# Mamba scan steps by turns in both channel halves, a gather of two 64-column products, three DRAM copies of the rows, and layer 1 in the same steps

## The chip, the cores and the metric

The kernel runs on one core of a Trainium2 chip, with its five engines: TensorE (PE, whose weight loads are shown as PEld), VectorE (DVE), ScalarE (ACT), GpSimd (POOL) and SyncE (SP, which here only issues DMAs). The metric is the device time in microseconds. Before the change it is 8173.62 us, the median of three runs (8168.15 to 8188.78).

## The reference: what is computed

An image x of two batches, 64 channels and 96 x 96 points goes through four layers:

- layer 0: attention over all 9216 points of a batch, added to x
- layer 1: depthwise and 1x1 convolutions, batch norm and ReLU; then a Mamba block over the 9216 points of each batch as one sequence
- layer 2: four Mamba blocks over the image's columns and rows (96 sequences of 96 points each way and batch, once forwards and once backwards), each direction pair joined by a linear layer
- layer 3: a 3 x 3 filter whose taps come from the image's mean

The change is in the Mamba blocks of layers 1 and 2. A block has 128 inner channels d and 16 states s. In each point t:

```
dt = softplus(...)                     # per channel and point
h[d,s] = exp(dt[d] * A[d,s]) * h[d,s] + dt[d] * B[s] * x[d]
y[d]   = sum over s of h[d,s] * C[s]  + x[d] * Dp[d]
```

B and C are the same for all channels of a point; dt and x the same for all states of a channel. In layer 1 h runs on from chunk to chunk; in layer 2 it starts from zero in each sequence. All is float32.

## The kernel before

**Units and steps.** A unit is one Mamba block on 768 points of one batch: 24 units in layer 1 (a chunk of 768 points each, with a carried state), 96 in layer 2 (eight sequences of 96 points, one direction; a forward and a backward unit of the same points follow each other and share the normalised input). 128 channels times 16 states are 2048 recurrences; 128 partitions hold 128 of them, so a unit has 16 steps. Partition p belongs to state p // 8 and, in step n, to channel (8n + p) mod 128: a step is eight channels for each state, and every step shifts the channels by eight partitions. (HALF = 384 points, CH = 768, STEPS = 16.)

**How the channels are shifted.** `step_write` (L821) writes the unit's tile dtu (128 channels x 1536: dt, and e = dt times x) to DRAM twice, one copy below the other, in two DMAs of 768 KB. `read` (L839) then fetches the 128 rows from row 8n on: the second copy makes the wrap. The SBUF tile that receives them is named spread; there are six, and a read is issued five steps ahead.

**One step of a unit.**

- `decay` (L849), ACT, three steps ahead: h = exp(dt times a rate per partition)
- `inputs` (L868), DVE: e times B into the PSUM tile place
- `scan` (L879): the DVE scan along the points, then on POOL h times C
- `gather` (L895), PE, two steps late: a 128 x 128 matrix of zeros and ones, a shifted window of the tile pair, sums the states of a channel into the PSUM tile low; one product per half of the points. Before the first of them a product with `direct` puts x times Dp there.
- `shared` (L859), PE: the product that gives B, in PSUM

Layer 1 (`carry` set) takes all 768 points of one group n in a step: one read of 768 KB, one decay, one scan whose first value is the carried state, which POOL copies back, and B in the tile that layer 2 uses for its second place. Layer 2 (`paired`) takes two groups n = 2m, 2m+1 on one half of the points in a step: steps 0 to 7 are the first half, 8 to 15 the second. It reads two blocks of 384 KB, has two decays of 384 points, and works out the inputs of two steps ahead of their two scans. In both layers a step has two gather products of 384 points.

**The other pieces of a unit** are worked in between. The list PIECES in `Mamba` gives each an offset in steps from the unit's step 0, and `run` (L998) issues, for every step: the read, the decay, inputs and scan, `shared`, the gather, then the pieces due. Every engine and the SP queue work their own instructions in exactly this order. The pieces that matter below, by the step at which they come up, whatever unit is being stepped through (call it j):

- 1, 5, 7, for unit j+1: `step_sum`, `step_dt`, `step_u` (POOL, L808, L811, L815): they finish dt and e. 8: `step_write` of them (SP, L824). From step 11 on the reads are those of unit j+1.
- 7, 9, for unit j+2: `conv_read` and `gate_read` (ACT, L765 and L772 to L774). 11, 13: `step_mm` (PE) and `step_read` (ACT, L791 and L792). 14: `step_exp` (ACT, L796 to L798). 15: `step_kept` (POOL, L805).
- 10: `y_half` (ACT, L915), which frees low for the second half of unit j. 3: `y_gate` (POOL, L926) of unit j-1.

So while unit j is stepped through, the dt and e of unit j+1 are finished, written out and read back shifted, and those of unit j+2 begun.

**DMA completions.** The SP queue's DMAs take eight completion semaphores in turn: a DMA is issued only when the one eight places before has landed.

Of the kernel before, what the change touches and what calls it, by code (L numbers as in the profile page):

```python
# [523 lines left out]
def mamba_tables(k, pool):  # L524

    nc = k.nc
    G = P // 8
    t = SimpleNamespace()  # L530

    t.member = pool.tile([P, 8], FP, name="member")
    nc.vector.reduce_sum(t.member, k.ident.rearrange("p (g i) -> p i g", i=8), axis=AX.X)
    t.group = pool.tile([P, 2, G], FP, name="group")
    for j in range(2):
        nc.vector.reduce_sum(t.group[:, j], k.ident.rearrange("p (g i) -> p g i", i=8), axis=AX.X)

    t.turned = pool.tile([P, G, G], FP, name="turned")
    two = t.group.rearrange("p j g -> p (j g)")
    for n in range(G):  # L540
        nc.vector.tensor_copy(t.turned[:, n], two[:, G - n : 2 * G - n])

    pair = pool.tile([P, 2, P], FP, name="pair")
    nc.vector.tensor_copy(pair, k.ident.unsqueeze(1).to_broadcast([P, 2, P]))
    pair = pair.rearrange("p j c -> p (j c)")
    t.gather = [pair[:, P - 8 * n : 2 * P - 8 * n] for n in range(G)]

    t.centre = pool.tile([P, P], FP, name="centre")
    nc.vector.tensor_sub(t.centre, k.ident, k.mean_c)
    return t  # L550
# [8 lines left out]
def mamba_weights(k, w, pool, product, tables, i):  # L559
# [15 lines left out]
    p = product(tables.placed.rearrange("p s i -> p (s i)"), tables.group[:, 0], P, G)  # L575
# [38 lines left out]
class Mamba:  # L614
# [14 lines left out]

    STEPS = P // 8  # L630
# [3 lines left out]
    def __init__(self, k, tables, wk, dram, ps, ps_m):  # L634
        self.k, self.nc, self.t = k, k.nc, tables
        self.wk, self.dram, self.ps_m = wk, dram, ps_m


        self.places = [self.wide(ps.tile([P, 2 * NB], FP, name=f"place{i}")) for i in range(2)]
        self.low = [ps.tile([P, NB], FP, name=f"low{i}")[:, :HALF] for i in range(2)]  # L640
# [141 lines left out]
    def step_read(self, u):  # L782
        nc = self.nc

        u.both = self.work("dtu", 2 * CH, bufs=1)
        order = "p (j a t) -> p a j t" if u.paired else "p (a j t) -> p a j t"
        both = u.both.rearrange(order, a=2, j=2)
        u.dt, u.e = both[:, 0], both[:, 1]
        u.kept = self.by_half(self.work("kept", bufs=1))
        p = self.by_half(u.p)  # L790
        nc.scalar.activation(u.e, p, AF.Abs, bias=u.w.dt_b)  # L791
        nc.scalar.activation(u.dt, p, AF.Relu, bias=u.w.dt_b)  # L792
# [28 lines left out]
    def step_write(self, u):  # L821
        u.rows = self.dram.tile([2 * P, 2 * CH], FP, tag="rows", name="rows")
        for j in range(2):
            self.nc.sync.dma_start(out=u.rows[j * P : (j + 1) * P], in_=u.both)  # L824
# [10 lines left out]
    def paired(self, step):  # L835
        half, m = divmod(step, self.STEPS // 2)
        return half, (2 * m, 2 * m + 1)

    def read(self, u, step):  # L839
        u.dtu[step] = self.work("spread", 2 * CH, bufs=6)  # L840
        if not u.paired:
            self.nc.sync.dma_start(out=u.dtu[step], in_=u.rows[8 * step : 8 * step + P])
            return
        half, groups = self.paired(step)
        for q, n in enumerate(groups):
            row = u.rows[8 * n : 8 * n + P, bass.ts(half, CH)]
            self.nc.sync.dma_start(out=u.dtu[step][:, bass.ts(q, CH)], in_=row)

    def decay(self, u, step):  # L849

        h = u.h[step] = self.work("h", bufs=9)
        if not u.paired:
            self.nc.scalar.activation(h, u.dtu[step][:, :CH], AF.Exp, scale=u.w.rates[:, step : step + 1])  # L853
            return
        for q, n in enumerate(self.paired(step)[1]):
            dt = u.dtu[step][:, q * CH : q * CH + HALF]
            self.nc.scalar.activation(h[:, bass.ts(q, HALF)], dt, AF.Exp, scale=u.w.rates[:, n : n + 1])  # L857

    def shared(self, u, half=0):  # L859

        if u.paired:
            sides, halves = [self.low[0]], [half]
        else:
            (sides, u.B), halves = self.places[1], range(2)
        for j, p in zip(halves, sides):
            self.nc.tensor.matmul(p, lhsT=u.w.bc[0], rhs=u.xc[:, bass.ts(j, HALF)], start=True, stop=True)  # L866

    def inputs(self, u, step):  # L868

        if not u.paired:  # L870
            u.bx = self.places[0][1]
            self.nc.vector.tensor_mul(u.bx, u.dtu[step][:, CH:], u.B)  # L872
            return
        bx = self.places[step % 2][1].rearrange("p (q t) -> p q t", q=2)
        x = u.dtu[step].rearrange("p (q a t) -> p q a t", q=2, a=2)[:, :, 1]
        B = self.low[0].unsqueeze(1).to_broadcast([P, 2, HALF])
        self.nc.vector.tensor_mul(bx, x, B)  # L877

    def scan(self, u, step):  # L879
        nc = self.nc  # L880
        h = u.h[step]
        if not u.paired:
            first = u.carry[:, step : step + 1]
            nc.vector.tensor_tensor_scan(h, h, u.bx, first, ALU.mult, ALU.add)  # L884
            nc.gpsimd.tensor_copy(first, h[:, CH - 1 :])  # L885
            nc.gpsimd.tensor_mul(h, h, u.C)  # L886
            return
        bx = self.places[step % 2][1]
        way = slice(None, None, -1) if u.rev else slice(None)
        nc.vector.tensor_tensor_scan(h[:, way], h[:, way], bx[:, way], 0.0, ALU.mult, ALU.add)  # L890
        h = h.rearrange("p (q t) -> p q t", q=2)
        C = u.C[:, bass.ts(self.paired(step)[0], HALF)]
        nc.gpsimd.tensor_mul(h, h, C.unsqueeze(1).to_broadcast([P, 2, HALF]))  # L893

    def gather(self, u, step):  # L895

        if u.paired:
            half, groups = self.paired(step)
            parts = [(half, self.low[1], q, n) for q, n in enumerate(groups)]
            begin, end = step % 8 == 0, step % 8 == 7  # L900
        else:
            parts = [(j, p, j, step) for j, p in enumerate(self.low)]
            begin, end = step == 0, step == self.STEPS - 1
        h = u.h[step]
        if begin:
            for half, p in {half: p for half, p, _, _ in parts}.items():
                self.nc.tensor.matmul(p, lhsT=u.w.direct, rhs=u.xc[:, bass.ts(half, HALF)], start=True, stop=False)  # L907
        for i, (_, p, q, n) in enumerate(parts):
            stop = end and (i == 1 or not u.paired)
            self.nc.tensor.matmul(p, lhsT=self.t.gather[n], rhs=h[:, bass.ts(q, HALF)], start=False, stop=stop)  # L910

    def y_half(self, u):
        if u.paired:
            u.y = self.work("yg")
            self.nc.scalar.copy(u.y[:, :HALF], self.low[1])  # L915

    def y_read(self, u):
        if u.paired:
            self.nc.scalar.copy(u.y[:, HALF:], self.low[1])
        elif not u.drained:  # L920
            u.y = self.work("yg")
            for j, p in enumerate(self.low):
                self.nc.scalar.copy(u.y[:, bass.ts(j, HALF)], p)
# [65 lines left out]
    @staticmethod  # L989
    def lates(now, s):  # L990
        halves = now and now[0].paired
        if s == 2 or (s == 10 and halves):
            return ()
        if s == 3 or (s == 11 and halves):
            return (3, 2)
        return (2,)

    def run(self, units, first, n_first, other):  # L998


        for u in units:
            u.dtu, u.h, u.paired, u.drained = {}, {}, not u.carry, False
# [5 lines left out]
        unit = lambda i: units[i] if i < len(units) else None  # L1008
# [16 lines left out]
        for n in range(begin, len(steps) + end + 1):  # L1025
# [5 lines left out]
            if at(n):  # L1031
# [3 lines left out]
                if not u.paired:  # L1035
                    self.inputs(u, s)
                elif s % 2 == 0:
# [3 lines left out]
                if u.paired and s == 6:  # L1041
                    self.shared(u, 1)
                if s == (14 if u.paired else 15) and unit(n // self.STEPS + 1):
                    after = unit(n // self.STEPS + 1)
                    if after.paired and not u.paired:

                        for late in (2, 1, 0):
                            self.gather(u, s - late)
                        self.y_read(u)
                        u.drained = True  # L1050
                    self.shared(after)
            if n == -1:
                self.shared(units[0])

            for late in self.lates(at(n), s):
                if at(n - late) and not (at(n - late)[0].drained):
# [297 lines left out]
```

## Time and profile before

| | us |
|---|---|
| median of three runs | 8173.62 |
| the profiled execution's own time | 8176.64 |
| its span, first to last instruction | 8174.9 |
| layer 0 and the filling of the first unit, to the first inputs of layer 1 | 2753 |
| layer 1, 24 units | 1182 (49.25 a unit) |
| layer 2, 96 units | 4156 (43.29 a unit) |
| layer 3 | 84 |

The stages are cut at the starts of the first L872 (layer 1's inputs), the first L877 (layer 2's inputs) and at the end of layer 2's last scans. Busy time of the span: PE 92%, DVE 83%, ACT 62%, POOL 58%; in layer 2 alone DVE 3896, POOL 3683, PE 3752 and ACT 2988 of 4156 us, and the 16 DMA engines 0.88 at 326 GB/s.

How to read it: busy time of an engine is time in which at least one of its instructions is at work. "x <- y" behind an idle time names what ended the wait. A timeline line has start, length, engine, line of the kernel, operation and tiles, and how many instructions follow each other there; idle time ahead of it stands in brackets. Lengths of neighbours overlap by some tens of ns. The granted clock (PEclk) is TensorE's, 1.00 being the full one. DMA share is the mean busy share of the 16 DMA engines.

### The profile page before, as it was taken

Reading aid. Unit: us, or ns where it says so; the run is one execution under the profiler, and the core shown is the slowest. Engines: PE = TensorE matmul, PEld = TensorE weight load, DVE = VectorE, ACT = ScalarE, POOL = GpSimd, SP = SyncE. Lnnn points to the kernel's source line nnn. Section 1 sums busy time; section 2 is a strip of 40 time slices with the busy share of each in tenths; the row PEclk is TensorE's granted clock in tenths of the full one; section 3 lists DMA queues with packets and bytes.
Section 4 is the critical chain, followed back from the end, with each engine's and each line's share of the span. In section 5 each row is a group of like instructions: output and inputs, shape, how many; then the busy total and the mean of one; then the engine's idle time right before and its main releaser. Section 6 shows DMA issues by size and latency. Waiting matters only on the chain.

```text
span 8174.9 us, 80364 instructions
## 1 busy us (share of the span) xinstructions
PE 7554.5 (92%) x24578; PEld 3358.0 (41%) x24578; DVE 6785.6 (83%) x5136; ACT 5045.4 (62%) x6473; POOL 4755.1 (58%) x3146
## 2 busy tenths in 40 slices
PE   9999999999999799999889998989999999999897
PEld 3333333333333344444444444444444444444443
DVE  6666666666666599988899999999999999999999
ACT  4444444444444566665676677777777777777774
POOL 0000000000000588888888888898999989888895
PEclk9999999999999798988999999999999999999999
DMA  1000000000000588777888888888898888888885
GB/s 42 1 1 1 1 1 1 3 4 4 4 4 5 205 294 296 284 286 277 292 315 317 317 321 333 330 324 331 334 337 328 330 336 336 331 321 334 324 329 211
DMA packets 538496, 1725.90 MB, mean 211 GB/s; under 512 B 59844, under 2 KB 60996, under 8 KB 537544
## 3 DMA queue, kind: packets, MB, share of 16 engines
q1 hardware_dynamic: 536608, 1717.66, 56.8%
q8 instruction: 194, 3.18, 0.2%
q10 hardware_dynamic: 1448, 3.05, 0.1%
q14 instruction: 246, 2.02, 0.1%
HBM read 1522.68 MB, written 197.79 MB: 210 GB/s over the span
## 4 chain that ended last, share of the span: by engine, by line
PE 21%; POOL 13%; issue 12%; ACT 8%; DMA 8%; DVE 4%; SPq 0%; DVEq 0%; ACTq 0%; POOLq 0%
PE low L910 10%; DMA spread<-rows 6%; POOL h L886 5%; POOL h L893 4%; PE mm L666 4%; ACT h L857 4%; PE conv L754 4%; DVE place L877 2%; DMA rows<-dtu 1%; PE low L907 1%; PE conv L748 1%; DVE h L890 1%; POOL dtu L811 1%; PE low L866 1%; ACT raw L773 1%
## 5 line engine op out<-in xcount | busy, mean ns | idle before, releaser
L910 PE MATMUL low<-h,pair 128*128 128x384 f32 x7680 | 2865.4, 515 | 44.2 <-POOL h L886 26.5
L893 POOL TENSOR_TENSOR h<-h,C 128x768 f32<-128x768 f32 x1536 | 2755.1, 1819 | 231.7 <-DVE h L890 225.1
L890 DVE TENSOR_TENSOR_SCAN h<-h,place 128x768 f32<-128x768 f32 x1536 | 2604.3, 1737 | 4.9 <-ACT h L857 4.9
L910 PEld LDWEIGHTS low<-h,pair 128*128 128x128 f32 x7680 | 1503.2, 201 | 1288.6 <-issue 270.7
L307 ACT ACTIVATE e<-f_exp 128x1536 f32<-128x1536 f32 x864 | 1207.1, 1449 | 1223.7 <-PE f_exp L297 1223.7
L363 DVE TENSOR_TENSOR acc_e<-acc_e,e 128x1536 f32<-128x1536 f32 x792 | 1389.9, 1755 | 684.5 <-ACT e L307 645.2
L857 ACT ACTIVATE h<-spread,xa 128x384 f32<-128x384 f32 x3072 | 1717.2, 607 | 368.7 <-DMA spread<-rows 336.8
L877 DVE TENSOR_TENSOR place<-spread,low 128x768 f32<-128x768 f32 x1536 | 1388.3, 949 | 251.0 <-PE low L866 238.4
L336 POOL TENSOR_TENSOR xa<-xa,t_att 64x512 f32<-64x512 f32 x36 | 45.4, 1261 | 2612.4 <-ACT t_att L334 2612.4
L314 PE MATMUL y_att<-e,xb 128*64 128x512 f32 x5184 | 1243.6, 601 | 0.0
L297 PE MATMUL f_exp<-theta,phi 64*128 64x512 f32 x5184 | 1234.4, 606 | 1.0 <-DVE xb L280 0.5
L297 PEld LDWEIGHTS f_exp<-theta,phi 64*128 64x128 f32 x5184 | 466.2, 186 | 754.6 <-issue 460.8
L884 DVE TENSOR_TENSOR_SCAN h<-h,state,place 128x768 f32<-128x768 f32 x384 | 696.1, 1813 | 67.7 <-ACT h L853 19.2
L886 POOL TENSOR_TENSOR h<-h,C 128x768 f32<-128x768 f32 x384 | 695.3, 1811 | 31.4 <-POOL state L885 1.0
L314 PEld LDWEIGHTS y_att<-e,xb 128*64 128x64 f32 x5184 | 341.5, 136 | 830.7 <-issue 829.3
L765 ACT ACTIVATE raw<-conv,cols 128x768 f32<-128x768 f32 x120 | 108.2, 901 | 886.1 <-PE conv L754 587.0
L754 PE MATMUL conv<-xn,xa 64*128 64x384 f32 (+3 forms) x1536 | 557.9, 503 | 16.6 <-DVE xa L1128 5.3
L872 DVE TENSOR_TENSOR place<-spread,place 128x768 f32<-128x768 f32 x384 | 369.1, 961 | 129.3 <-PE place L866 116.9
L853 ACT ACTIVATE h<-spread,rates 128x768 f32<-128x768 f32 x384 | 351.1, 931 | 175.0 <-DMA spread<-rows 173.6
L907 PE MATMUL low<-raw,xa 128*128 128x384 f32 x384 | 220.2, 662 | 257.8 <-ACT yg L915 175.6
L754 PEld LDWEIGHTS conv<-xn,xa 64*128 64x128 f32 x1536 | 277.6, 190 | 286.7 <-issue 98.7
L805 POOL TENSOR_TENSOR kept<-dtu,kept 128x768 f32<-128x768 f32 x120 | 218.2, 1819 | 285.1 <-ACT kept L798 285.1
(207 smaller groups left out, 6041.4 us busy)
## 6 DMA issues: line engine op xcount, KB each, us to landing
spread<-rows SPq DMA_DIRECT2D x3072, 384.0 KB, 6.4
spread<-rows SPq DMA_DIRECT2D x384, 768.0 KB, 4.5
rows<-dtu SPq DMA_DIRECT2D x240, 768.0 KB, 5.8
image<-pre SPq DMA_DIRECT2D x11, 384.0 KB, 2.3
xb<-image SPq DMA_DIRECT2D x11, 384.0 KB, 7.9
xa<-in_x SPq DMA_DIRECT2D x1, 2304.0 KB, 22.2
out<-xa ACTq DMA_DIRECT2D x7, 240.0 KB, 2.0
out<-xa SPq DMA_DIRECT2D x1, 1200.0 KB
```

The lines of the kernel that those rows point to most:

```text
L297: nc.tensor.matmul(fs[j // 3][:, bass.ts(j % 3, NB)], lhsT=phi[at, bass.ts(m // 2, P)], rhs=theta[at, bass.ts(i, NB)], start=True, stop=True,)
L307: nc.scalar.activation(e, f, AF.Exp)
L314: nc.tensor.matmul(y[rows_of(m % 2)], lhsT=g[:, m, :], rhs=es[j // 3][:, bass.ts(j % 3, NB)], start=m < 2, stop=m >= KEYS - 2,)
L363: nc.vector.tensor_add(acc, acc, e)
L754: self.nc.tensor.matmul(p3[:, :, o], lhsT=lhsT, rhs=x3[:, :, i], **flags)
L857: self.nc.scalar.activation(h[:, bass.ts(q, HALF)], dt, AF.Exp, scale=u.w.rates[:, n : n + 1])
L877: self.nc.vector.tensor_mul(bx, x, B)
L884: nc.vector.tensor_tensor_scan(h, h, u.bx, first, ALU.mult, ALU.add)
L886: nc.gpsimd.tensor_mul(h, h, u.C)
L890: nc.vector.tensor_tensor_scan(h[:, way], h[:, way], bx[:, way], 0.0, ALU.mult, ALU.add)
L893: nc.gpsimd.tensor_mul(h, h, C.unsqueeze(1).to_broadcast([P, 2, HALF]))
L910: self.nc.tensor.matmul(p, lhsT=self.t.gather[n], rhs=h[:, bass.ts(q, HALF)], start=False, stop=stop)
```

## The change

- A step covers both halves of the channels, 0 to 63 and 64 to 127 (q = 0, 1), on one half of the points. In turn n (0 to 7) partition p holds channel 64q + (8n + p) mod 64. Steps 0 to 7 are the eight turns of the first half of the points, 8 to 15 those of the second.
- The shift now wraps within 64 channels, and 128 partitions are read: each half of the channels lies in DRAM three times. `step_write` issues six DMAs of 64 rows (384 KB each) in place of two of 128 rows (768 KB each). The two reads of a step are 128 rows of 768 floats as before.
- The gather's matrix is 128 x 64, and the two products of a step go to the upper and the lower 64 rows of the PSUM tile y. Their count stays.
- Layer 1 takes the same steps: two reads of 384 KB for one of 768 KB, two decays of 384 points for one of 768, two scans of 384 points, each from its own carried state, for one of 768, the inputs of two steps ahead of their scans. The special code between the layers goes.
- The tables for rates and gather are built to match (some small DVE instructions at the start).

The order of the pieces is that of layer 2 before, now for both layers. In all, the kernel issues 3840 reads for 3456, 720 writes for 240, and 384 more instructions each on DVE and ACT; the counts of PE and POOL do not change.

```diff
     def step_write(self, u):
-        u.rows = self.dram.tile([2 * P, 2 * CH], FP, tag="rows", name="rows")
-        for j in range(2):
-            self.nc.sync.dma_start(out=u.rows[j * P : (j + 1) * P], in_=u.both)
+        u.rows = self.dram.tile([6 * C, 2 * CH], FP, tag="rows", name="rows")
+        for q in range(2):
+            for at in range(3 * q * C, 3 * (q + 1) * C, C):
+                self.nc.sync.dma_start(out=u.rows[at : at + C], in_=u.both[rows_of(q)])
...
     def read(self, u, step):
+        half, turn = self.turn(step)
         u.dtu[step] = self.work("spread", 2 * CH, bufs=6)
-        if not u.paired:
-            self.nc.sync.dma_start(out=u.dtu[step], in_=u.rows[8 * step : 8 * step + P])
-            return
-        half, groups = self.paired(step)
-        for q, n in enumerate(groups):
-            row = u.rows[8 * n : 8 * n + P, bass.ts(half, CH)]
-            self.nc.sync.dma_start(out=u.dtu[step][:, bass.ts(q, CH)], in_=row)
+        for q in range(2):
+            at = 3 * q * C + 8 * turn
+            self.nc.sync.dma_start(out=u.dtu[step][:, bass.ts(q, CH)], in_=u.rows[at : at + P, bass.ts(half, CH)])
...
     def scan(self, u, step):
...
+        if u.carry:
+            state = u.carry[:, 2 * turn : 2 * turn + 2]
+            for q in range(2):
+                at = bass.ts(q, HALF)
+                nc.vector.tensor_tensor_scan(h[:, at], h[:, at], bx[:, at], state[:, q : q + 1], ALU.mult, ALU.add)
+            nc.gpsimd.tensor_copy(state.unsqueeze(2), h2[:, :, HALF - 1 :])
+        else:
+            way = slice(None, None, -1) if u.rev else slice(None)
+            nc.vector.tensor_tensor_scan(h[:, way], h[:, way], bx[:, way], 0.0, ALU.mult, ALU.add)
...
     def gather(self, u, step):
...
+        half, turn = self.turn(step)
+        if turn == 0:
+            self.nc.tensor.matmul(self.y, lhsT=u.w.direct, rhs=u.xc[:, bass.ts(half, HALF)], start=True, stop=False)
+        for q in range(2):
+            rhs, stop = u.h[step][:, bass.ts(q, HALF)], turn == self.STEPS // 2 - 1
+            self.nc.tensor.matmul(self.y[rows_of(q)], lhsT=self.t.gather[turn], rhs=rhs, start=False, stop=stop)
```

## The prediction

> **What bounds the kernel now.** I read the page first (PE 92% busy, DVE 83%), then the three stages by windows, then the waits, then one unit of layer 2 on the timeline, since that layer is 4156 of the 8174.9 us. Counted in 768-point units, it takes 4156/96 = 43.29 us a unit. The waits of the whole run, engines and then SP's queue:
>
> ```profile
> ACT h L857 <- DMA spread<-rows: 336.8, 629, 4.3
> POOL kept L805 <- ACT kept L798: 285.1, 100, 25.4
> DVE place L877 <- PE low L866: 238.4, 99, 5.2
> SPq L824 <- POOL dtu L819: 736.1, 95, 10.0
> ```
>
> Once a unit, each of four queues waits for another: DVE for PE's B, POOL for ACT, ACT for reads, and SP's write for POOL. The third line tempts: a lighter PE would give DVE up to 238 us back. But the others close a ring. One turn of it, from a unit's write to the next unit's write (SP, ACT, POOL, SP):
>
> ```profile
> 6065.62 0.80 SPq L824 DMA_DIRECT2D rows<-dtu  x2
> ...
> 6072.97 0.61 ACT L857 ACTIVATE h<-spread,xa 128x384 f32<-128x384 f32 x1 [0.80 <-DMA spread<-rows]
> ...
> 6078.58 0.61 ACT L857 ACTIVATE h<-spread,xa 128x384 f32<-128x384 f32 x1 [0.31 <-DMA spread<-rows]
> 6079.22 0.90 ACT L791 ACTIVATE dtu<-mm,cols 128x768 f32<-128x768 f32 x1
> ...
> 6083.56 0.94 ACT L798 ACTIVATE kept<-kept,minus 128x768 f32<-128x768 f32 x1
> ...
> 6084.57 1.83 POOL L805 TENSOR_TENSOR kept<-dtu,kept 128x768 f32<-128x768 f32 x1 [2.12 <-ACT kept L798]
> ...
> 6105.89 1.80 POOL L815 TENSOR_TENSOR dtu<-dtu,raw 128x768 f32<-128x768 f32 x1
> 6107.75 0.11 POOL L819 MEMSET dtu<- 128x8 f32 x1
> ...
> 6107.89 0.80 SPq L824 DMA_DIRECT2D rows<-dtu  x2
> ```
>
> Behind the write (6065.62) stand the reads of steps 14 and 15 and the next unit's step 0, in the same DMA queue. ACT's decays wait for them in its program order, and step_read (L791) and step_exp (to L798) stand behind those decays. POOL's kept (L805) waits for step_exp; from there to step_u (L815) POOL works thirteen instructions of 1.8 us without a gap, and then SP may write again. Write to kept is 18.95 us, kept to the next write 23.32. Over layer 2's units, the starts of these instructions give 18.97 from a forward unit's write and 23.4: a turn of 42.35. From a backward unit's write it is 20.8, since step_mm comes late on PE there; over both the turn is the 43.29 of the stage. So the ring sets layer 2's time, PE's lateness costs it only 43.29 - 42.35 = 0.94 us a unit, and **whatever lengthens the write lengthens the ring one for one**.
>
> The DMA windows, with these columns last: granted clock, DMA share, GB/s. The first three rows are that turn (before the write, the write, the reads behind it); the last two are the load of x, first from 64-partition transfers, then one of 128:
>
> ```profile
> 6061.00:6065.00 4.00, 4.00 (x13) 1.75 (x11) 4.00 (x4) 2.64 (x5) 4.00 (x3) 1.00 0.25 99
> 6066.00:6070.00 4.00, 4.00 (x12) 1.53 (x11) 4.00 (x4) 3.95 (x4) 4.00 (x3) 1.00 0.94 343
> 6072.00:6080.00 8.00, 8.00 (x23) 4.04 (x23) 8.00 (x7) 6.13 (x9) 5.45 (x4) 1.00 1.03 407
> 20.00:26.00 6.00, 6.00 (x74) 3.33 (x68) 3.62 (x10) 2.53 (x4) 0.00 (x0) 1.00 0.98 206
> 31.00:33.00 2.00, 2.00 (x26) 1.05 (x24) 1.01 (x3) 1.21 (x2) 0.00 (x0) 1.00 0.97 415
> ```
>
> The DMA engines idle while SP waits for POOL, then are full for the write and the reads behind it. A load into 64 partitions keeps them as busy (0.98) and moves half as much.
>
> **The change, part by part.**
>
> *The write (cost).* Two DMAs of 768 KB are 1.573 MB: 4.6 us at 343 GB/s. Six of 384 KB are 2.359 MB, and each comes from 64 partitions, first three from the lower half, then three from the upper. The trace has no store from 64 partitions, so I bound it: at the store's own 343 GB/s it lasts 6.9 us; at half of that, 172, 13.7. The nearest rows in form are the 64-partition loads: 206 GB/s for rows of 18 KB (above), and 243 from 14 to 16 us for rows of 6 KB like these, in alternating halves. I take 223: 10.6 us, **6.0 more** than now. SP's four further issues (0.4 us each) lie within the transfers. Behind the write stand SP's reads of steps 14, 15, 0 and 1, so ACT's decays, step_exp, and POOL: the ring.
>
> The Trainium skill (SBUF — State Buffer, section "Door 1: The DMA port swizzle (why `[64,N]` ≈ `[32,N]`)") says that partitions 0 to 63 reach only eight of sixteen ports, about 218 GB/s; the 206 against 415 above agrees. By that figure the write would take an estimated 10.8 us, and the sum below would rise by some 25 us.
>
> *The gather (gain).* The timeline has PE's full 128 x 128 products at eight instructions in 6080.83 - 6078.25 = 2.58 us, so a step's four take 1.29. Layer 0's side-by-side 128 x 64 products run twelve of 512 columns in 2.75 us (1488.45 to 1493.95 for two such groups). Per instruction and column that is 0.45 ns against 0.84. Four of 384 columns alone would be 0.65 at half of 1.29, 0.7 by layer 0's rate, and up to 1.0 if both changes of form cost 0.17 (2.75 less 12 x 512 x 0.42 ns). So PE gains 0.3 to 0.6 us a step, 5 to 10 a unit, and step_mm is on time. On the ring that is worth the 0.94, no more; what is late next is the reads.
>
> The skill's page TensorEngine Tiling (Array Packing), section "Key Properties", speaks against the pairs: changing the tiling mode drains TensorE. The 0.17 above holds one such change per group of twelve; two drains a step leave the gain at its lower end, and since PE would be off the ring the sum is the same by either.
>
> *DVE and ACT in layer 2.* Nothing changes in count or shape. DVE's own pace is two steps in 5.01 us, 40.1 a unit, under the ring.
>
> *Layer 1.* Now 1182/24 = 49.25 us a unit. DVE paces it there: inputs and scan alternate every 2.94 us (timeline, L872 to L872), 47.0 for 16 steps. After, two inputs precede the scans as in layer 2 (2.5), and two scans of 384 replace one. The split costs between nothing (half of 1.81 each) and 0.26 (a whole small DVE instruction, L589's of 128 x 128), so at most 2.8 a step: 44 a unit, under the ring. POOL's thirteen (23.4) plus eight state copies (0.18 and a gap of 0.09 each) are 25.6 from kept to write, measured now 26.3; I take 26.0. Write to kept is layer 2's 18.97 plus 0.4 for norm_affine, which stands between those decays. ACT's second decay (2 x 0.53 for 0.88, 0.2 a step) lies within its waits. The ring is 45.4 + 6.0 = 51.4, **2.15 more** than now.
>
> *The rest.* Sixteen small table instructions lie beside layer 0. The first unit's fill grows by its write, 6.
>
> **The sum**, on the profiled execution's own 8176.64 us (span 8174.9 and 1.7 around it; 3 above the median of the runs):
> - layer 2: 42.35 + 6.0 - 43.29 = 5.06, x 96 = +486
> - layer 1: 2.15 x 24 = +52; first fill +6
> - 8176.64 + 544 = 8721, so **8720 us**
>
> **Rivals.**
> - *The stores go at their full rate* (6.9 us, +2.3). For it: only loads were seen slow. Layer 2: 44.65, +131; layer 1: 47.7, -37; 8176.64 + 94 = 8270.
> - *Faster: the two halves' stores run beside each other.* All six DMAs stand in the queue together; if the engines spread so that both halves move at once, 2 x 206 = 412 GB/s, 5.7 us, +1.1: layer 2 43.45 (+15), layer 1 46.5 (-66), 8125. It decides from 6.1 us: 120 units times the excess equal 0.94 x 96 + 3.85 x 24 = 182 there. Against it: layer 0's two loads into opposite halves, queued together, moved 206.
> - *Stores at half of 343* (13.7 us, +9.1): 3.1 x 120 over my sum, 9090.
> - *The clock falls.* An idler PE may get half the clock, as in the first fill (2654 to 2753: 0.57). PE's way from y_half through step_mm, 3.5 us then (a product of 0.65, two pairs, 1.3), would double; the longer write leaves it that room, so this matters only with the two short writes.
>
> **Chances.** Mine 0.60, with a range of its own of 8580 to 8960 (write 9.4 to 12.6 us, 120 us per us). Full-rate 0.20, side by side 0.14, half the store's rate 0.06. The range takes in my case and the full-rate one, 8260 to 8960, and leaves out 0.20. About 0.3% is what a measurement of this kernel tells from no change: faster 0.13, same 0.02, slower 0.85.
>
> **What would show it.** Right: units of 48 us in layer 2 at equal spacing; a DMA share near 1 but only some 220 GB/s after each write for 10 us; more of "ACT h <- DMA spread<-rows" (some 6 us a unit more), and no "DVE place <- PE". The gather's group at half its busy time with nothing gained. Wrong: write to kept still 19 us (the halves ran together), or kept to write shorter than 23 (POOL's row of thirteen is not fixed); or a unit near 40, DVE's own pace, which would mean that the ring gives way.

## The result and the profile after

The changed kernel takes 8909.08 us, the median of four runs (8901.92 to 8911.30), against 8181.20 (8168.15 to 8192.35) for the kernel before, run beside it: 1.089 times as long, with a 95% interval of 1.087 to 1.091. The execution profiled below took 8901.92 us, with a span of 8900.0.

Line numbers have moved: the write is now L829, the read L849, the decay L858, the inputs L868, the side-by-side gather L893; step_read to step_exp are L795 to L802, kept L809, step_u L819 with its memset L823. First the waits, engines and then SP's queue:

```profile
ACT h L858 <- DMA spread<-rows: 1399.2, 1062, 10.8
DVE place L868 <- DMA spread<-rows: 939.2, 238, 9.0
DVE place L868 <- PE B L862: 218.3, 91, 85.9
POOL kept L809 <- ACT kept L802: 197.7, 101, 25.0
...
SPq L829 <- POOL dtu L823: 771.3, 95, 9.2
```

The waits for spread have grown, now to 10.8 us at a time, and DVE too now waits for reads, 939 us in all. Its wait for PE's B is nearly gone from layer 2: the third line holds one wait of 85.9 us, and between 4100 and 8800 us the same view gives 64.8 in all, where the kernel before has 232.9 in its layer 2. SP's write still waits for POOL once a unit.

One turn of the ring in the new timeline (SP, ACT, POOL, SP; the answers for single engines put together in order of time):

```profile
6108.61 8.05 SPq L829 DMA_DIRECT2D rows<-dtu  x6
...
6115.12 0.46 ACT L897 COPY yg<-y 128x384 f32<-128x384 f32 x1
6123.11 0.61 ACT L858 ACTIVATE h<-spread,xa 128x384 f32<-128x384 f32 x1 [7.54 <-DMA spread<-rows]
6125.72 0.61 ACT L858 ACTIVATE h<-spread,xa 128x384 f32<-128x384 f32 x1 [1.99 <-DMA spread<-rows]
...
6130.08 0.88 ACT L795 ACTIVATE dtu<-mm,cols 128x768 f32<-128x768 f32 x1
...
6134.40 0.94 ACT L802 ACTIVATE kept<-kept,minus 128x768 f32<-128x768 f32 x1
...
6135.41 1.83 POOL L809 TENSOR_TENSOR kept<-dtu,kept 128x768 f32<-128x768 f32 x1 [1.41 <-DVE h L883]
...
6156.64 1.85 POOL L819 TENSOR_TENSOR dtu<-dtu,raw 128x768 f32<-128x768 f32 x1
6158.54 0.11 POOL L823 MEMSET dtu<- 128x8 f32 x1
...
6158.68 2.39 SPq L829 DMA_DIRECT2D rows<-dtu  x3
```

In this turn the view names DVE's scan as the end of kept's wait; ACT's L802 ends in the same moment (6134.40 + 0.94), and from 4000 us on it is ACT that ends 76 of the 95 waits of kept. From the write (6108.61) to kept (6135.41) it is 26.80 us, from kept to the next write (6158.68) 23.27. The first leg has grown by 7.85 us on this turn, and nearly all of it stands ahead of the first two decays behind the write, where ACT is idle for 7.54 and 1.99 us (0.80 before the change, in the line shown, and 0.32 for the decay after it). The second leg is as it was. What the transfers did meanwhile is in the windows (last columns: granted clock, DMA share, GB/s), before the write, in it, in the 4 us behind it, and later:

```profile
6104.00:6108.00 4.00, 3.75 (x14) 1.70 (x13) 4.00 (x4) 1.62 (x3) 4.00 (x3) 1.00 0.06 24
6110.00:6120.00 10.00, 4.71 (x15) 1.31 (x11) 7.96 (x6) 5.53 (x6) 9.84 (x7) 0.71 0.98 215
6120.00:6124.00 4.00, 3.45 (x14) 1.45 (x12) 0.00 (x0) 0.61 (x1) 1.60 (x1) 0.88 0.95 280
6124.00:6132.00 8.00, 3.27 (x8) 1.27 (x10) 5.25 (x5) 4.90 (x8) 1.59 (x1) 0.74 0.99 368
```

For ten microseconds the DMA engines are full and move 215 GB/s; in the write before the change it was 343 for 4.

Over layer 2's steady units of both traces (means; the legs by the starts of these instructions, the unit of layer 2 by the starts of its first inputs, the unit of layer 1 as that stage divided by 24, the write by its packets from the first to the last):

| us | before | after |
|---|---|---|
| unit in layer 2 | 43.19 | 50.01 |
| write to kept | 19.80 (18.99 and 20.63 by turns) | 26.62 (26.78 and 26.44) |
| kept to the next write | 23.43 | 23.41 |
| the write: MB, us, GB/s | 1.573, 5.13, 307 | 2.359, 11.57, 204 |
| unit in layer 1 | 49.58 | 52.94 |
| PE busy in a unit of layer 2 | 39.2 | 34.3 |

The two legs make up the unit by definition (to 0.04 us, since it is taken from other starts), so their sum proves nothing. What carries weight is that one leg kept its length to 0.02 us while the other took up all of the 6.82 us. Layer 2 gives 6.82 x 96 = 655 us, layer 1 3.36 x 24 = 81; together 736, where the two profiled executions are 725 us apart.

### The profile page after: what moved, and what is told of

Read it like the earlier page. It is cut to its first block, busy times and chain, and to the rows that moved or that the text cites. A ratio compares the mean times of both kernels' runs of the same rounds, so it can differ in the third digit from the quotient of the medians.

```text
span 8900.0 us, 82743 instructions
## 1 busy us (share of the span) xinstructions
PE 6957.1 (78%) x24578; PEld 2475.4 (28%) x24578; DVE 6769.6 (76%) x5523; ACT 5125.6 (58%) x6857; POOL 4747.4 (53%) x3146
## 3 DMA queue, kind: packets, MB, share of 16 engines
q14 instruction: 262, 2.15, 0.1%
## 4 chain that ended last, share of the span: by engine, by line
DMA 14%; SPq 13%; POOL 13%; ACT 7%; issue 6%; PE 5%; DVE 3%; POOLq 0%; DVEq 0%; ACTq 0%
DMA spread<-rows 14%; POOL h L884 8%; SPq L829 8%; SPq L849 5%; ACT h L858 3%; POOL dtu L819 2%; PE mm L671 2%; POOL dtu L815 2%; PE y L893 1%; DVE place L868 1%; DVE h L883 1%; DVE xa L1216 1%; PE conv L753 1%; ACT dtu L796 1%; ACT kept L801 1%
## 5 line engine op out<-in xcount | busy, mean ns | idle before, releaser
L868 DVE TENSOR_TENSOR place<-spread,B 128x768 f32<-128x768 f32 x1920 | 1745.7, 949 | 1157.7 <-DMA spread<-rows 939.2
L858 ACT ACTIVATE h<-spread,xa 128x384 f32<-128x384 f32 x3072 | 1740.6, 608 | 1222.6 <-DMA spread<-rows 1211.2
L893 PE MATMUL y<-h,pair 128*64 128x384 f32 x7680 | 1822.8, 601 | 44.4 <-POOL h L884 44.0
L893 PEld LDWEIGHTS y<-h,pair 128*64 128x64 f32 x7680 | 546.4, 163 | 1235.3 <-issue 867.7
L671 PE MATMUL mm<-raw,xa 128*128 128x384 f32 x768 | 409.0, 668 | 502.2 <-ACT xb L929 475.6
L879 DVE TENSOR_TENSOR_SCAN h<-h,state,place 128x384 f32<-128x384 f32 x768 | 715.3, 992 | 24.3 <-issue 21.8
L890 PE MATMUL y<-raw,xa 128*128 128x384 f32 x384 | 272.9, 808 | 533.4 <-ACT yg L897 272.8
L858 ACT ACTIVATE h<-spread,rates 128x384 f32<-128x384 f32 x768 | 428.7, 607 | 201.6 <-DMA spread<-rows 188.0
L862 PE MATMUL B<-raw,xa 128*128 128x384 f32 x384 | 205.7, 622 | 261.9 <-DVE place L868 261.8
L671 PEld LDWEIGHTS mm<-raw,xa 128*128 128x128 f32 x768 | 179.7, 260 | 754.0 <-ACT xb L929 506.4
```

What stands on the lines that cost most here:

```text
L671: self.nc.tensor.matmul(o, lhsT=lhsT, rhs=x, start=n == 0, stop=n == len(terms) - 1)
L868: self.nc.vector.tensor_mul(bx, x, self.B.unsqueeze(1).to_broadcast([P, 2, HALF]))
L879: nc.vector.tensor_tensor_scan(h[:, at], h[:, at], bx[:, at], state[:, q : q + 1], ALU.mult, ALU.add)
L893: self.nc.tensor.matmul(self.y[rows_of(q)], lhsT=self.t.gather[turn], rhs=rhs, start=False, stop=stop)
```

## The experiments

Theory: the ring of the prediction (write, reads behind it, ACT, POOL) sets the unit, and the write got long because its stores come from 64 partitions. Rivals: it is the third copy's bytes; the six DMAs and SP's issuing; the granted clock, which fell from 0.955 to 0.869; the new gather. All but the last four, on the later write, are one execution each, beside runs of the kernel before of 8180.1 us (the first four) and 8169.35 us (the next four); the last four are timed several times, with intervals.

**The bytes alone.** The kernel before, with a third copy of 128 partitions.

```diff
-        u.rows = self.dram.tile([2 * P, 2 * CH], FP, tag="rows", name="rows")
-        for j in range(2):
+        u.rows = self.dram.tile([3 * P, 2 * CH], FP, tag="rows", name="rows")
+        for j in range(3):
             self.nc.sync.dma_start(out=u.rows[j * P : (j + 1) * P], in_=u.both)
```

> The kernel before, with a third DMA of 768 KB from all 128 partitions behind the two writes of each unit (nobody reads it). Ring theory (a unit lasts from its write to kept and from kept to the next write; what lengthens the write lengthens the unit): the write grows from 5.1 to 7.7 us, write to kept from 19.8 to about 21.6, kept to write stays at 23.4; layer 2 some 45.0 us a unit (+160 to 170 in all), layer 1 0 to +2.6 a unit; 8340 to 8410 us. Volume theory (the bytes written are what cost, from whatever partitions): as many bytes as the changed kernel, so most of its loss, over 8800. Clock theory (the idler PE with its lower granted clock is what cost): PE has the same work as before, so 8180 and little more.

8336.67 us, 157 more than before. The write of the same 2.359 MB as after's lasts 6.99 us (338 GB/s), 1.86 more than two copies; the unit of layer 2 is 44.43 (+1.24), kept to write 23.45. That is a little less than expected, since the write grew by 1.86 and not by 2.6.

**The partitions alone.** The kernel before, its two copies written in four DMAs of 64 partitions: no byte more.

```diff
         for j in range(2):
-            self.nc.sync.dma_start(out=u.rows[j * P : (j + 1) * P], in_=u.both)
+            for q in range(2):
+                at = j * P + q * C
+                self.nc.sync.dma_start(out=u.rows[at : at + C], in_=u.both[rows_of(q)])
```

> The kernel before, its two writes of 128 partitions cut into four of 64 (first both copies of the lower half, then both of the upper); the bytes stay. Ring theory with half the rate from 64 partitions: 1.573 MB at 204 GB/s are 7.7 us for 5.1, so the same as with a third copy: write to kept about 21.6, 8340 to 8410 us. Volume theory: no change, 8180. Clock theory: no change, 8180.

8503.05 us, 323 more than before, twice the price of the third copy. The same 1.573 MB now take 7.64 us instead of 5.13: 206 GB/s. The unit is 46.07, kept to write 23.44. I had expected 8340 to 8410, as for the third copy. The write is as long as expected, but after a forward unit write to kept grows by 3.69 (to 22.67) and the write by 2.51 only. After a backward unit write to kept is 22.63: the two kinds of unit no longer differ, although PE has its old gather.

**The third copy and the new gather, without 64-partition stores.** The changed kernel with its halves taken as even and odd channels: three DMAs of all 128 partitions, and a read fetches every second row of DRAM. The weights, A_log and the matrices of the gather's end are put in that order.

```diff
-        for q in range(2):
-            for at in range(3 * q * C, 3 * (q + 1) * C, C):
-                self.nc.sync.dma_start(out=u.rows[at : at + C], in_=u.both[rows_of(q)])
+        for j in range(3):
+            self.nc.sync.dma_start(out=u.rows[j * P : (j + 1) * P], in_=u.both)
...
-            at = 3 * q * C + 8 * turn
-            self.nc.sync.dma_start(out=u.dtu[step][:, bass.ts(q, CH)], in_=u.rows[at : at + P, bass.ts(half, CH)])
+            rows = u.rows.rearrange("(r q) t -> q r t", q=2)[q]
+            row = rows[8 * turn : 8 * turn + P, bass.ts(half, CH)]
+            self.nc.sync.dma_start(out=u.dtu[step][:, bass.ts(q, CH)], in_=row)
```

> The changed kernel with the channels split into even and odd ones in place of lower and upper: the three copies can then be three DMAs of all 128 partitions (768 KB), and the reads take every second row. The order of the A, gate and out-projection weights on the host and the direct matrix follow. Same bytes, same steps, same half-width gather. Ring theory: the write is that of the kernel with a third copy, 7.0 us, write to kept 18.99 + 1.9 = 20.9, kept to write 23.4: 44.3 us a unit in layer 2, 47 to 48 in layer 1, 8220 us (8180 to 8300), so nearly all of the change's loss goes and the gather's gain shows as the 0.9 us a unit by which PE was late. Volume theory: the bytes are the same, 8909. If every second row reads slower, in between.

8213.18 us: 696 less than the changed kernel with the same bytes, the same number of reads and the same gather. The write takes 6.97 us (339 GB/s), the unit 43.90 (43.19 before), and in layer 1 47.79 (49.58 before). Its window from the write, with DMA share and GB/s last, and behind it that of the four half stores:

```profile
6024.00:6029.00 5.00, 0.35 (x4) 0.00 (x0) 5.00 (x5) 4.94 (x5) 5.00 (x4) 1.00 1.05 404
6030.00:6034.00 4.00, 4.00 (x11) 0.93 (x10) 3.08 (x3) 1.23 (x2) 4.00 (x4) 0.50 0.96 376
```

```profile
6018.00:6024.00 6.00, 2.81 (x9) 1.40 (x8) 6.00 (x7) 5.94 (x7) 5.92 (x4) 0.95 0.93 213
6025.00:6029.00 4.00, 4.00 (x7) 2.04 (x7) 2.34 (x2) 0.62 (x1) 4.00 (x3) 0.50 0.95 284
```

The first row of each is the write, the second the reads just behind it. The half stores move 213 GB/s at a share of 0.93, and the reads behind them are slow too. As means over layer 2's units, the 4 us behind the write move 301 GB/s after the change and 308 with the four half stores, but 413, 409 and 409 in the kernel before, with the third copy alone and with all partitions; 4 us later all are at 386 or more. That is 4 x (413 - 301) / 405, some 1.1 us, lost to the reads.

**The number of DMAs.** The changed kernel with each half's three copies in one DMA, so two issues instead of six.

```diff
-            for at in range(3 * q * C, 3 * (q + 1) * C, C):
-                self.nc.sync.dma_start(out=u.rows[at : at + C], in_=u.both[rows_of(q)])
+            out = u.rows[3 * q * C : 3 * (q + 1) * C].rearrange("(j r) t -> r j t", j=3)
+            self.nc.sync.dma_start(out=out, in_=u.both[rows_of(q)].unsqueeze(1).to_broadcast([C, 3, 2 * CH]))
```

> The changed kernel with the three copies of a half in one DMA (64 partitions, each row read three times): two DMAs of 1152 KB for six of 384. In the changed kernel write to kept grew by 7.6 us over a forward unit's 18.99 while the write grew by 6.4: 1.2 us lie elsewhere. If they come from six small DMAs (SP takes 6.2 us to issue them, and they hold six of the eight completion semaphores), they go: 48.8 us a unit, 8765 us. If they belong to the 64 partitions (the reads behind the write run slower for some microseconds, in the kernel with four half stores too), nothing changes: within 60 us of 8909. The ring itself is not touched: kept to write 23.4.

8920.76 us, as after. The first to the last issue are 0.64 us apart instead of 6.22, the write takes 11.55 us at 204 GB/s and write to kept is 26.75. So the slow issues of the six cost no time. The 4 us behind the write move 319 GB/s, so the slow reads are not those of six DMAs either.

**The order of the halves.** The changed kernel with the writes of the lower and upper half by turns.

```diff
-        for q in range(2):
-            for at in range(3 * q * C, 3 * (q + 1) * C, C):
+        for j in range(3):
+            for q in range(2):
+                at = (3 * q + j) * C
```

> The changed kernel, its six writes in the order lower, upper, lower, upper half of the partitions in place of three lower, then three upper. If the queue lets neighbours of different halves move at once, the write falls from 11.6 us towards 7, and the unit with it: 8250 to 8400 us. If the transfers are worked in turn whatever half they come from, the write stays at 11 to 12 us and the time within 60 us of 8909. I expect the second, as in layer 0's loads into opposite halves.

8733.36 us, 176 less than after, which I had not expected: the write takes 10.19 us at 231 GB/s, so opposite halves do run beside each other a little where their DMAs are neighbours in the queue, far from the 412 of the "side by side" rival over the whole write. The Trainium skill (SBUF — State Buffer, section "Can I just issue two DMAs to hit both halves?") gives +6% for two DMAs into opposite halves over a single one; here it is 231 / 204, +13%, and a run further down shows more.

**The gather undone.** The changed kernel with 128-column gather matrices that hold zeros for the other half.

```diff
-            self.nc.tensor.matmul(self.y[rows_of(q)], lhsT=self.t.gather[turn], rhs=rhs, start=False, stop=stop)
+            self.nc.tensor.matmul(self.y, lhsT=self.t.wide[turn][q], rhs=rhs, start=False, stop=stop and q == 1)
```

> The changed kernel with its gather products 128 columns wide again (the other 64 are zeros), so PE has the work that it had before the change. Ring theory: PE is off the ring, so the units stay at 50.0 us in layer 2 and the whole within 30 us of 8909, while PE's gather group goes from 1823 us busy to about 2850. Clock theory: the granted clock comes back from 0.87 towards 0.95 and the time falls by some hundreds of us. A theory by which the gather's gain was real but spent elsewhere: slower by up to 0.6 us x 16 x 120 = 1150 us.

8945.93 us, 37 more than after and just outside the 30 expected. The gather's group (the time before the comma is in all, the one behind it the mean ns of one) in the changed kernel and in this one:

```profile
L893 PE MATMUL y<-h,pair 128*64 128x384 f32 x7680 | 1822.8, 601 | 44.4 <-POOL h L884 44.0
```

```profile
L893 PE MATMUL y<-h,xa 128*128 128x384 f32 x7680 | 2943.4, 529 | 16.8 <-POOL h L884 14.3
```

PE is given 1120 us more to do, and 37 of them reach the end. The granted clock rises to 0.931 with the busier PE, 1231 us at half clock instead of 2327, and nothing is gained by it: the clock rival falls. The kernel that turns out fastest below has 1597 us at half clock.

**POOL's leg shortened.** If the ring is right, a shorter second leg must gain time too. In the changed kernel and in the kernel before, step_sum, step_dt and step_u come at the unit's steps 0, 1 and 2 instead of 1, 5 and 7.

```diff
-        (-15, "step_sum"),
-        (-11, "step_dt"),
-        (-9, "step_u"),
+        (-16, "step_sum"),
+        (-15, "step_dt"),
+        (-14, "step_u"),
```

> The changed kernel with step_sum, step_dt and step_u on POOL at steps 0, 1 and 2 in place of 1, 5 and 7; the write stays at step 8 of SP's order. Between kept and the write POOL then has six instructions for thirteen, so kept to write falls from 23.4 to 11 or to where SP itself comes to the write, and the ring no longer binds. Ring theory: the next bound is the DMA engines, 33 us of reads and 11.6 of write a unit: 45 to 46 us a unit in both layers, 8280 to 8450 us. Volume theory: the DMA engines were the bound already, 8909. Clock theory: no change, 8909.

> The kernel before with step_sum, step_dt and step_u on POOL at steps 0, 1 and 2 in place of 1, 5 and 7. Ring theory: the ring that set layer 2 before the change is opened there too; next are DVE (40.5 us busy a unit) and PE's lateness, which then falls on DVE: 41 to 42 us a unit in layer 2, layer 1 at DVE's 47 to 48, so 7900 to 8060 us. If DVE waiting for PE's B was the bound and not the ring: no change, 8180.

The changed kernel takes 8479.24 us, 430 less, just above what I expected. Kept to write falls by 8.2 us to 15.25, but write to kept grows by 4.2 to 30.8. The kernel before becomes slower: 8502.91 us, 334 more, though kept to write falls there too, to 16.06: write to kept grows from 19.80 to 31.0. The ring opened, but my forecast of what comes next was wrong.

In the changed kernel the write itself also got faster: 9.34 us, 253 GB/s, with the same six DMAs in the same order. It is now issued while reads still stand ahead of it in the queue; its first packet comes 4.2 us after the first issue instead of 1.11. Two windows within one write (DMA share and GB/s last):

```profile
5999.00:6002.00 3.00, 3.00 (x12) 1.31 (x10) 3.00 (x3) 0.41 (x1) 3.00 (x2) 1.00 1.03 407
6003.00:6006.00 3.00, 2.54 (x12) 0.83 (x10) 3.00 (x4) 2.98 (x5) 2.88 (x2) 1.00 0.99 223
```

So the rate of "side by side" does occur, for some 3 us: as means over layer 2 the stores move 355 to 397 GB/s from their second to their fourth us, and some 210 later. That stores of both halves are then at work at once fits this, but no run shows why. 64-partition stores are slow here in the queue as it stood in the changed kernel, not in every one.

In the kernel before, DVE stands for PE's B more than twice as long as it did (558.6 us against 238.4):

```profile
DVE place L877 <- PE low L866: 558.6, 184, 5.6
```

One such wait, PE and then DVE in the same trace:

```profile
6023.48 1.56 PE L910 MATMUL low<-h,pair 128*128 128x384 f32 x4 [1.43 <-POOL h L893]
6027.21 1.56 PE L910 MATMUL low<-h,pair 128*128 128x384 f32 x4 [2.17 <-POOL h L893]
6028.70 5.40 PE L754 MATMUL conv<-xn,xa 64*128 64x384 f32 x8
6034.03 1.65 PE L866 MATMUL low<-raw,xa 128*128 128x384 f32 x2
...
6035.72 1.83 DVE L877 TENSOR_TENSOR place<-spread,low 128x768 f32<-128x768 f32 x2 [4.91 <-PE low L866]
```

POOL now works one piece after every h, so it gives PE one step's h every 3.6 us; with a piece after every second h it would be two in 5.4 (each instruction is 1.8). PE's gathers wait for them in order, and the product for B (L866), which needs nothing from POOL, stands behind them. DVE then idles 4.91 us. But POOL's order is not all of it. Between the gathers and B stand the eight products L754, which take 5.40 us here; the same eight take 2.81 in the kernel before (second line), and the granted clock was 0.55 meanwhile (first line, third column from the end):

```profile
6028.00:6034.00 6.00, 6.00 (x11) 2.63 (x9) 2.80 (x2) 0.00 (x0) 6.00 (x4) 0.55 0.94 293
```

```profile
6012.22 2.81 PE L754 MATMUL conv<-xn,xa 64*128 64x384 f32 x8
```

At the full clock these products and B's two (1.65 us here, 0.91 in the kernel before) would be some 3.3 us shorter, an estimate from these lines: most of the 4.91. So the bunched pieces sent the delay round by another way, POOL, PE, DVE, and the lower clock made it longer; how the 334 us divide between the two was not tested.

**The write put later, behind the reads it holds up.** step_write at step 10 instead of 8, so that two more steps' reads stand ahead of it, and step_u where it was. POOL's row is not touched. In the kernel before and in the one with all partitions:

```diff
-        (-8, "step_write"),
+        (-6, "step_write"),
```

> The kernel before with step_write two steps later in SP's order, at 10 in place of 8: POOL has the data no earlier or later, but SP now issues the reads of steps 14 and 15 ahead of the write, in the time in which it waited for POOL, and the next unit's reads follow the write directly. POOL's order is untouched. Ring theory: write to the landing of the next unit's first read loses two steps' reads (4 us) and gains the wait for the write's landing (some 1.7), so the ring falls from 42.35 to about 40 us after a forward unit; after a backward unit PE's late step_mm stays, so 41.5 to 42.5 on average and 8000 to 8130 us. If the ring is not what binds: 8170 to 8190.

> The kernel with even and odd channels (three writes of all 128 partitions, x7_all_partitions, 8213 us, 43.9 us a unit), and step_write at 10 in place of 8. Ring theory: PE is not late here, so the whole 2.2 us come off the ring: 41.7 us a unit in layer 2, 46 to 47 in layer 1, 7950 us (7900 to 8060). If the ring is not what binds: 8213.

The kernel before gains a little: 8121.83 us (8116.42 to 8130.40, four runs), 0.993 of before with an interval of 0.991 to 0.994. Write to kept is 19.15, 0.65 less. All partitions with the later write takes **7965.33 us** (7960.06 to 7971.13, four runs), 0.974 of before (0.972 to 0.975), and beats both kernels. It is 248 us below the earlier write, in units of 41.60. Its waits, engines and then SP:

```profile
ACT h L859 <- DMA spread<-rows: 350.0, 664, 4.7
DVE place L869 <- PE B L863: 228.9, 106, 89.0
...
SPq L829 <- POOL dtu L824: 268.5, 95, 3.8
```

Both times lie in the ranges expected, but with all partitions PE is late again, which I had not expected: ACT's step_read waits 83.8 us for it (7.8 with the earlier write, 75.6 in the kernel before). SP's write waits 2.8 us a unit for POOL instead of 8.1 with the earlier write (772.2 over 95 waits). DVE is busy 40.6 of the 41.6 us: here the ring and DVE's own pace stand within 1 us of each other.

**The later write with POOL's leg shortened moderately**, step_dt and step_u at steps 3 and 5:

```diff
-        (-11, "step_dt"),
-        (-9, "step_u"),
+        (-13, "step_dt"),
+        (-11, "step_u"),
```

> The kernel before this one with step_dt and step_u on POOL at steps 3 and 5 in place of 5 and 7, spread and not bunched as in the early_u kernels: two of POOL's instructions fewer between kept and the write. Ring theory: 3.6 us off the ring, which falls under DVE's 40.6, so DVE binds at 41 to 41.5 us a unit: 7850 to 7950 us. The other way: POOL's pieces again hold back h, PE's gathers wait for h and B comes late, as in x4_early_u and x8_before_early_u, where DVE waited for B twice a unit: then as the kernel with the write at 10, or slower.

> The kernel before with the write at 10 and step_dt and step_u at 3 and 5. With the ring open on both sides PE's lateness is what is left, and the full-width gather shows its price: 41.5 to 43 us a unit, 8000 to 8150 us, so slower than the kernel with the half-width gather in the same order by some 100 us. If the gather is worth nothing even then: the same as that kernel.

All partitions: 8009.44 us (8001.15 to 8020.69), 44 more than without it. Kept to write is 20.58, 2.8 less, but write to kept grows by 3.2 to 21.47. The kernel before: 8122.48 us (8100.96 to 8143.66), the same as without it. The two are 113 us apart, about the 100 expected, but neither gained by it. A shorter leg of POOL is worth nothing there any more, so the ring doesn't set the time alone; which of DVE's pace, PE's order and the reads does was not followed further.

## Why the prediction was right

- **The ring** held. Kept to write was predicted to stay at 23.4 and is 23.4 in the kernel before, after, and in every variant that left POOL's pieces alone (23.38 to 23.60), whatever the write lasted. The first leg took all the rest.
- **The write, +6.0 us**, was +6.44 (5.13 to 11.57), at 204 GB/s where I took 223. Here two misses partly cancel, which is luck: the new write lasted 0.97 longer than my 10.6, but the old one too 0.53 longer than my 4.6, which came from a window inside it and not from end to end. I chose between the 206 of rows of 18 KB and the 243 of rows of 6 KB that alternate; the stores stand at the lower one. Alternating them gave 231, so the row that I let pull the value up owed its excess, as far as the runs show, to its alternating halves, not to its 6 KB.
- **The term that was missing: the reads behind the write.** I let them run at their old pace. Write to kept came to 26.62 where 18.97 + 6.0 = 24.97 was predicted: 0.44 us are the write, 1.21 the reads, which move 301 GB/s for 4 us instead of 413 (worth some 1.1 by the estimate above). This comes with 64-partition stores, whether there are two, four or six, and not with 128-partition ones at the same place in the queue. Why, the runs don't settle; nothing tried separates the stores' own tail from what the reads do.
- **Layer 2, +486** became 655: (0.44 + 1.21) x 96 = 158, and 10 from the unit of before, 43.19 in steady units against the 43.29 I took from the stage. The stage was cut 7 us early: the first L877 starts at 3942.26, not at 3935.
- **Layer 1, +2.15 a unit** became +3.36, for the same reasons: write to kept 26.65 against 25.4, kept to write 26.49 against 26.0. By the same cut, layer 1 before was 49.58 a unit and not 49.25. The split scan cost 0.17 us a step (two of 992 ns for one of 1813), within my 0 to 0.26 and, as stated, under the ring. The first fill did not grow by 6: the first inputs start at 2752 us before and at 2750 after.
- **The gather's gain** came about on PE and was worth next to nothing. Its group fell from 2865 to 1823 us, a factor of 0.64. The half I named is nearly there at full clock, 0.196 us busy per product for 0.354; but 2331 of the 7680 products began at half clock, for 527 before. PE's busy time fell 4.9 us a unit, the lower end of my 5 to 10. Taking it back costs 37 us in 8909.
- **The 0.94 for PE being on time** came, but not from the gather, so here the sum was right by luck. Write to kept is 26.78 and 26.44 by turns where it was 18.99 and 20.63; yet it evens out with the full-width gather as well, at 22.67 and 22.63 with the four half stores and 26.90 and 26.52 with the gather undone, and there ACT's step_read waits 5.2 and 9.6 us in all for PE (75.6 before, 8.3 after). So the longer write alone is enough. With a write of 7 us the lighter gather does help: 20.72 and 20.34 with all partitions, 20.53 and 21.54 with the third copy alone.
- **The rivals.** "Full rate" (8270) has its price about right: at 339 GB/s the three copies give 8213 with the new gather. The price of "side by side" (8125) was not met by any run: 412 GB/s came only for part of a write, in the kernel with POOL's leg shortened. In the changed kernel the stores go at neither rate. "Half the store's rate" by 343 is also off: 204 is between half and the whole of it, and two thirds of the 307 that the old write had from end to end.
- **What would show it**: 215 GB/s for 10 us after each write is there, as is the end of most of DVE's waits for PE. The units came at 50.0, not 48. ACT's wait for spread grew by more than 6, (1211 - 337) / 96 = 9.1 us a unit, since ACT has no more work in the 6.8 us by which the unit is longer, and now waits for reads where it waited for others.

The cost is therefore not the third copy as such. On its own it costs 157 us, 64-partition stores on their own 323; both together, where every extra byte goes at the low rate, and with the new gather and layer 1's new steps, 728. With stores from all partitions the change comes within 0.6% of the kernel before (8213 against 8169, one execution of it), and it is 123 less than the kernel before with the third copy, whose write is as long (8337). With the write moved behind two more steps of reads it is 7965 against 8122 for the same move in the kernel before. In the two profiled executions 84 us of this lie in layer 2 and 72 in layer 1, whose steps changed as well (47.1 us a unit against 50.1). That the ring had kept PE's gain from being seen fits this, but is not shown: the later write with all partitions and the full-width gather was not run.

## What to carry to other kernels

Where no engine is full, look for a ring: list for each in-order queue what stands ahead of the wait, and follow it round to where it began; the legs' lengths, taken from starts of instructions, tell what an edit is worth better than any busy share. Before an edit splits a tile by partitions, price its stores from a row with the same partitions, not the same bytes, and add the reads that stand behind them. When a leg is shortened, ask what each engine then does in order: the same three pieces of POOL, moved early, went with a gain of 430 us in one kernel and a loss of 334 in the other.

## What the runs showed of the hardware

- A write to DRAM from 64 partitions went at 204 to 206 GB/s, whether as two, four or six DMAs, and at 231 with the halves by turns; from 128 at 306 to 319 (two DMAs) and 338 to 356 (three). Issued while reads still stood ahead of them in the queue, the same six 64-partition DMAs went at 253 over the whole write and at 355 to 397 from their second to their fourth us.
- Reads that stand behind a 64-partition write moved 278 to 319 GB/s in their first 4 us, against 409 to 413 behind writes of 128 partitions in three kernels. In the kernel before with POOL's pieces at steps 0, 1 and 2 it was 358 behind such a write, and with the later write 262 to 320, so partitions alone do not set it.
- The first to the last of the write's six issues on SP were 6.22 us apart; taking them down to two, 0.64 apart, gained nothing (8921 against 8909).
- Reads of every second row of DRAM were no slower than reads of neighbouring rows: their packets took 32.4 us a unit against 33.0 and 33.3.
- The clock granted to PE was at half for 2327 us in the changed kernel and 739 before, and cost no time there that the runs can show: with 1231 the kernel was no faster (8946), and the fastest (7965) had 1597. Where DVE stood waiting for PE's B it did count: eight products took 5.40 us at 0.55 in place of 2.81.
